# Pairwise bilinear products: one VectorE multiply over two PSUM banks, third product two halves later

## The chip, the cores and the metric

The kernel runs on one core of a Trainium2 chip. The metric is the time of one execution in microseconds on the device; lower is better. TensorE (PE in the profile) does the matrix products and writes PSUM, ScalarE (ACT) and VectorE (DVE) read and write PSUM and SBUF, GpSimd (POOL) works in SBUF, and the DMA moves data between HBM and SBUF. DMAs are issued from the queues of SyncE (SP), ScalarE and GpSimd.

## The reference

There are 1024 rows with 32 fields of 128 numbers each. For each of the 496 pairs of fields i < j there is a 128 x 128 matrix; field i is multiplied by it, and the result is multiplied element by element with field j. Everything is float32.

```python
# r_inputs: (1024, 32, 128), L0_rec_W: (496, 128, 128)
_pairs = list(itertools.combinations(range(32), 2))
v_i = inputs[:, I_IDX, :]
v_j = inputs[:, J_IDX, :]
transformed = jnp.einsum('bpd,ped->bpe', v_i, W)
return transformed * v_j
```

## The kernel before

**Tiles.** Each field is held transposed, 128 partitions (d) by 1024 columns (the rows of the batch). A pair q has one 128 x 128 weight and an output of 128 x 1024. It is worked in two halves of 512 columns; u = 2q + h numbers the halves. One half's product fills one PSUM bank (128 x 512 float32), and there are eight banks: `ppool` holds eight tiles of one bank each.

**Order of pairs.** Pairs run row by row from i = 30 down to i = 0, and in a row over j = i+1 to 31, so the first rows are short and the last is 31 pairs long.

**Three products.** The first 15 pairs (`nq0`) use one float32 matmul per half (line 209). All others use three quicker fp32r products. A weight w is split into a high part `wh`, a rest `wl` and a difference `wd`, and a field into `xh`, `xl` and `xd`. Half u goes through these steps:

1. `first(u)`: two matmuls on TensorE into its bank, `wh` by `xh` and `wl` by `xl` (line 212); then ScalarE scales the bank in place by 1 + 2^-12 (line 213).
2. `second(u)`, which runs LAG = 3 halves later in the order: the third matmul, `wd` by `xd`, adds to the bank (line 221); then VectorE multiplies the bank with field j and writes the output tile (line 227).

**The loop.** The order of all instructions is written out by hand (`manual_schedule`). For each u the loop calls `first(u)`, loads that fall due, `second(u - LAG)`, stores that fall due, and, at odd u, at most one split; the `xd` subtractions put down in `later` come last. Each engine works its instructions in this order; a wait holds up everything behind it on that engine.

**Splits.** `split_w` takes two pairs' weights at a time (128 x 256): ScalarE makes `wh` (line 127), GpSimd makes `wl` and `wd` (lines 128 to 130), in four buffers per kind. `split_x` takes half a field: ScalarE `xh` (line 142), GpSimd `xl` (lines 143 and 144), and `xd` either on GpSimd (line 148) or, for 16 fields, on VectorE through `later` (line 265), due at `min(u + XDLAG, 2*first_q[f] + LAG - 1)`.

**Output.** Four pairs share an output tile (2 MB, `out_tile`). There are seven slots for such tiles at first: three of their own (`s0` to `s2`) and four that will later hold groups of fields (`g0` to `g3`). These four are given up one after the other, ahead of the group loads at pairs 52, 141, 219 and 313 (20 pairs earlier each); from then on three are left. VectorE can't write a tile before the store that last used its slot has landed. A full tile is stored by one DMA from ScalarE's queue (line 258), SLAG = 2 halves after `second` of its last half in the order; the first four pairs and the last four are stored pair by pair, and the last two pairs in halves.

**Loads.** Weights come eight pairs at a time (512 KB, line 118) into three buffers, fields singly (512 KB, line 90) or in groups of four (2 MB, line 108), nearly all from SyncE's queue. Seven of the later weight loads go out in two parts, 112 partitions from GpSimd's queue and 16 from SyncE's (lines 102 and 103), with small DMAs (`mark`, line 99) around them.

Of the kernel before, what the change touches and what calls it, by code (L numbers as in the profile page):

```python
# [7 lines left out]
F32 = mybir.dt.float32  # L8
F32R = mybir.dt.float32r
ALU = mybir.AluOpType  # L10

P = 128
NF = 32
NQ = NF * (NF - 1) // 2
BT = 1024
HB = 512
WC = 2
WL = 8
OG = 4
EPS = 2.0**-12  # L20
NATIVE = 5
SHARED = 16
XDLAG = 10
LAG = 3
WB = 3
WLEAD = 12
XAFTER = 54
# [7 lines left out]
XAT = (313, 219, 141, 52)  # L35
OWAIT = 20
SLAG = 2


def _pairs():  # L40
# [5 lines left out]
def kernel(  # L46
# [22 lines left out]
    nc = tc.nc  # L69
# [5 lines left out]
    rpool = ctx.enter_context(tc.tile_pool(name="wr", bufs=WB))  # L75
    wpool = ctx.enter_context(tc.tile_pool(name="ws", bufs=4))
    opool = ctx.enter_context(tc.tile_pool(name="o", bufs=1))
    ppool = ctx.enter_context(tc.tile_pool(name="ps", bufs=8, space=bass.MemoryType.PSUM))

    x_sb = {}  # L80

    def load_x(f, pieces=1, eng=None):
        if f == 0:

            t = rpool.tile([P, WL, P], F32, tag="w", name="x_0").rearrange("p q e -> p (q e)")
        else:
            t = xpool.tile([P, BT], F32, tag=f"x{f}", name=f"x_{f}")
        s = BT // pieces
        for k in range(pieces):
            (eng or nc.sync).dma_start(out=t[:, k * s : (k + 1) * s], in_=xt[f, :, k * s : (k + 1) * s])  # L90
        x_sb[f] = t

    w_raw = {}
# [18 lines left out]
    def load_w(c, splits=(0, WL), eng=nc.sync):  # L112
# [4 lines left out]
        for a, b in zip(splits, splits[1:]):  # L117
            eng.dma_start(out=w_raw[c][:, a:b, :], in_=wt[c, :, a:b, :])

    w_s = {}  # L120

    def split_w(c, u):

        k = c * WC % WL
        raw = w_raw[c * WC // WL][:, k : k + WC, :].rearrange("p q e -> p (q e)")
        h, l, d = [wpool.tile([P, WC * P], F32R, tag=t, name=f"{t}_{c}") for t in ("wh", "wl", "wd")]
        nc.scalar.mul(h, raw, 1.0 - 2.0**-13)  # L127
        nc.gpsimd.tensor_tensor(l, raw, h.bitcast(F32), ALU.subtract)  # L128
        nc.gpsimd.tensor_scalar(d, h.bitcast(F32), EPS, 1.0, ALU.mult, ALU.mult)  # L129
        nc.gpsimd.tensor_tensor(d, l.bitcast(F32), d.bitcast(F32), ALU.subtract)  # L130
        w_s[c] = (h, l, d)

    x_s = {}
    later = []

    def split_x(f, a, u):
# [8 lines left out]
        if f > NF - 2 - NATIVE - SHARED:  # L145
            later.append((min(u + XDLAG, 2 * first_q[f] + LAG - 1), d, h.bitcast(F32), l.bitcast(F32)))
        else:
# [9 lines left out]
    for c in range(c0, nchunk):  # L157
        todo.append(((c - 3) * WC + 1, max(c * WC, nq0), lambda u, c=c: split_w(c, u)))
# [33 lines left out]
    def out_tile(g):  # L192
        t = min((t for t in used if (g + 1) * OG <= until.get(t, NQ + OG)), key=used.get)
        used[t] = g
        pool = xpool if t in until else opool
        return pool.tile([P, OG, BT], F32, tag=t, name=f"ot_{g}")

    ctx.enter_context(tc.manual_schedule())
    po, ots, stores = {}, {}, []


    def first(u):
        q, h = divmod(u, 2)
        i, c = pairs[q][0], q // WC
        r = slice(q % WC * P, (q % WC + 1) * P)
        s = slice(h * HB, (h + 1) * HB)
        po[u] = ppool.tile([P, HB], F32, tag="po", name=f"po_{u}")
        if q < nq0:
            nc.tensor.matmul(po[u], w_raw[q // WL][:, q % WL, :], x_sb[i][:, s], start=True, stop=True)  # L209
        else:  # L210
            for t in (0, 1):
                nc.tensor.matmul(po[u], w_s[c][t][:, r], x_s[i][t][:, s], start=t == 0, stop=t == 1)  # L212
            nc.scalar.mul(po[u], po[u], 1.0 + EPS)  # L213

    def second(u):
        q, h = divmod(u, 2)
        i, j = pairs[q]
        r = slice(q % WC * P, (q % WC + 1) * P)
        s = slice(h * HB, (h + 1) * HB)
        if q >= nq0:  # L220
            nc.tensor.matmul(  # L221
                po[u], w_s[q // WC][2][:, r], x_s[i][2][:, s], start=False, stop=True, skip_group_check=True
            )
        g, k = divmod(q, OG)
        if k == 0 and h == 0:
            ots[g] = out_tile(g)
        nc.vector.tensor_tensor(ots[g][:, k, s], po.pop(u), x_sb[j][:, s], ALU.mult)  # L227
        if q >= NQ - 2:
            stores.append((u + SLAG, out[g, :, k, s], ots[g][:, k, s]))
        elif g == 0 or q >= NQ - OG:  # L230
            if h == 1:
                stores.append((u + SLAG, out[g, :, k], ots[g][:, k]))
        elif k == OG - 1 and h == 1:
            stores.append((u + SLAG, out[g], ots[g]))

    for u in range(2 * NQ + LAG + SLAG):
        q = u // 2
        if u < 2 * NQ:
            i, j = pairs[q]
            if u % 2 == 0 and j == i + 1 and XG * ngroup < i - 2 - XLEAD:  # L240
                load_x(i - 2 - XLEAD)
            first(u)
            if u == 2 * nq0:
                move_on(5)
            if u % 2 == 0 and q in group_at:
                load_group(group_at[q])
            if u % 2 == 1 and q in w_at:
                load_w(w_at[q])
                if w_at[q] in WAPART:
                    back.append(q + BACK)  # L250
            if u % 2 == 0 and q in back:
                move_on(16 - NE if q < w_q[WAPART[-1]] else 13)
            if u == 2 * x_at + 1:
                load_x(0)
        if LAG <= u < 2 * NQ + LAG:
            second(u - LAG)
        while stores and stores[0][0] <= u - LAG:
            nc.scalar.dma_start(*stores.pop(0)[1:])
        if u % 2 == 1:
            ready = [t for t in todo if t[0] <= q]  # L260
            if ready:
                ready[0][2](u)
                todo.remove(ready[0])
        while later and later[0][0] <= u:
            nc.vector.tensor_tensor(*later.pop(0)[1:], ALU.subtract)  # L265
# [33 lines left out]
```

## Time and profile before

| | |
|---|---|
| runs | 754.4, 752.0, 750.39, 753.91 us; median 752.95 |
| profiled execution | 754.4 us in all, span 752.6 us |
| mean granted TensorE clock | 0.984 of full speed |
| DMA | 310.05 MB, mean 412 GB/s; HBM written 260.05 MB, read 49.29 MB |
| stores | 122 of 2048 KB, 13.4 us from issue to landing in the median |
| weight loads from SyncE | 54 of 512 KB, 10.8 us |
| field group loads | 4 of 2048 KB, 18.7 us |
| ScalarE xh (line 142) | 52 operations, 32.6 us |
| GpSimd wl, wd (lines 128 to 130) | 3 x 241 operations, 758, 416 and 740 ns |
| longest waits | wl on wh 78.1 us (78 times); scaling on products 54.0 (44); multiply on stores 45.7 (33) |

The span is the time from the first to the last instruction of the profiled execution; the other runs have only a total. A group's row gives how often it ran, its busy time, the mean duration of one, the idle time of the engine just ahead of it and what ended most of that idle time. Matmuls overlap: one lasts 0.39 us in the records, while they start 0.23 us apart. So TensorE's busy share is not its distance from a limit. Idle time of an engine that something else holds up costs nothing by itself.

### The profile page before, as it was taken

The numbers are of one execution on the slowest core, as the hardware profiler recorded it, in microseconds if no ns is written. First come the engines' busy times: TensorE is split into PE (matmuls) and PEld (weight loads), VectorE is DVE, ScalarE is ACT, GpSimd is POOL, SyncE is SP. The second block draws the span as 40 slices with busy tenths as digits, with TensorE's granted clock in tenths as the row PEclk, the third lists the DMA queues.
The fourth block names the chain that finished last, engine by engine and source line by source line (L and its number), as shares of the span: only waits on it lengthen the run. The fifth ranks groups of instructions, "written<-read, shape, count | busy, mean of one in ns | idle before, by whom it ended". The sixth has DMA issues, their size and how long they took to land.

```text
span 752.6 us, 10976 instructions
## 1 busy us (share of the span) xinstructions
PE 703.5 (93%) x2946; PEld 554.9 (74%) x2946; DVE 655.4 (87%) x1024; ACT 625.5 (83%) x1256; POOL 591.5 (79%) x866
## 2 busy tenths in 40 slices
PE   7998999999999997998999979989999999998994
PEld 3576777778888776776787758768777787777883
DVE  3999999999998995977889859879898989887995
ACT  1298989999999987787898868889998898887993
POOL 1789999999988788486988866878888979796761
PEclk9999999999999999899999998999999999999998
DMA  9999999999999999999999997999999999999998
GB/s 345 425 425 429 412 428 426 428 423 426 426 416 428 426 429 427 398 419 422 412 429 404 417 391 299 391 432 426 420 418 428 403 427 402 427 426 395 392 430 353
DMA packets 31789, 310.05 MB, mean 412 GB/s; under 512 B 3952, under 2 KB 4080, under 8 KB 15600
## 3 DMA queue, kind: packets, MB, share of 16 engines
q10 hardware_dynamic: 19584, 261.10, 82.5%
q1 hardware_dynamic: 10880, 45.03, 15.2%
q0 software_dynamic: 1264, 3.22, 1.3%
q8 instruction: 24, 0.39, 0.2%
q14 instruction: 37, 0.30, 0.1%
HBM read 49.29 MB, written 260.05 MB: 411 GB/s over the span
## 4 chain that ended last, share of the span: by engine, by line
PE 55%; DMA 22%; POOL 11%; DVE 8%; issue 2%; ACT 1%; DVEq 0%; ACTq 0%; POOLq 0%
PE po L212 35%; DMA out_dram<-ot 22%; PE po L221 17%; DVE ot L227 7%; PE po L209 4%; POOL xl L143 2%; POOL wl L128 2%; POOL xd L148 2%; POOL wd L130 2%; POOL xl L144 1%; POOL wd L129 1%; DVE xd L265 1%; DMA x<-in_xt_dram 1%; ACT po L213 0%; ACT wh L127 0%
## 5 line engine op out<-in xcount | busy, mean ns | idle before, releaser
L213 ACT ACTIVATE po<-po 128x512 f32<-128x512 f32 x962 | 545.2, 583 | 94.9 <-PE po L212 54.0
L227 DVE TENSOR_TENSOR ot<-po,x 128x512 f32<-128x512 f32 x720 | 459.4, 683 | 69.9 <-DMA out_dram<-ot 39.4
L212 PE MATMUL po<-xh,wh 128*128 128x512 f32 x962 | 380.4, 395 | 22.0 <-DVE ot L227 21.9
L212 PE MATMUL po<-xl,wl 128*128 128x512 f32 x962 | 378.9, 394 | 11.0 <-POOL wl L128 9.7
L221 PE MATMUL po<-xd,wd 128*128 128x512 f32 x962 | 376.9, 392 | 1.8 <-DVE xd L265 0.9
L128 POOL TENSOR_TENSOR wl<-w,wh 128x256 fp32r<-128x256 f32 x241 | 182.6, 758 | 81.4 <-ACT wh L127 78.1
L212 PEld LDWEIGHTS po<-xh,wh 128*128 128x128 f32 x962 | 182.0, 189 | 70.7 <-DVE ot L227 32.2
L212 PEld LDWEIGHTS po<-xl,wl 128*128 128x128 f32 x962 | 182.1, 189 | 54.1 <-POOL wl L128 15.5
L221 PEld LDWEIGHTS po<-xd,wd 128*128 128x128 f32 x962 | 182.0, 189 | 41.0 <-ACT po L213 2.4
L130 POOL TENSOR_TENSOR wd<-wl,wd 128x256 fp32r<-128x256 f32 x241 | 178.3, 740 | 20.1
L227 DVE TENSOR_TENSOR ot<-po,x_g 128x512 f32<-128x512 f32 x272 | 172.1, 684 | 18.5 <-PE po L212 7.5
L129 POOL TENSOR_SCALAR wd<-wh 128x256 fp32r<-128x256 f32 x241 | 100.2, 416 | 20.4
L127 ACT ACTIVATE wh<-w 128x256 fp32r<-128x256 f32 x241 | 99.3, 413 | 7.2 <-DVE ot L227 5.4
L143 POOL TENSOR_TENSOR xl<-x_g,xh 128x512 fp32r<-128x512 f32 x32 | 41.4, 1295 | 0.0
L143 POOL TENSOR_TENSOR xl<-x,xh 128x512 fp32r<-128x512 f32 x20 | 26.3, 1314 | 16.2 <-ACT xh L142 16.0
L144 POOL TENSOR_SCALAR xl<-xl 128x512 fp32r<-128x512 f32 x52 | 34.9, 671 | 4.6
L209 PE MATMUL po<-x,w 128*128 128x512 f32 x60 | 30.4, 669 | 4.0 <-DMA x<-in_xt_dram 4.0
L265 DVE TENSOR_TENSOR xd<-xh,xl 128x512 fp32r<-128x512 f32 x32 | 30.2, 944 | 0.0
L209 PEld LDWEIGHTS po<-x,w 128*128 128x128 f32 x60 | 12.4, 212 | 21.3 <-issue 14.0
L148 POOL TENSOR_TENSOR xd<-xh,xl 128x512 fp32r<-128x512 f32 x20 | 25.9, 1293 | 1.7
L142 ACT ACTIVATE xh<-x 128x512 fp32r<-128x512 f32 x20 | 12.4, 628 | 11.5 <-DMA x<-in_xt_dram 11.4
L142 ACT ACTIVATE xh<-x_g 128x512 fp32r<-128x512 f32 x32 | 20.2, 630 | 0.0
(7 smaller groups left out, 11.2 us busy)
## 6 DMA issues: line engine op xcount, KB each, us to landing
out_dram<-ot ACTq DMA_DIRECT2D x122, 2048.0 KB, 13.4
w<-in_wt_dram SPq DMA_DIRECT2D x54, 512.0 KB, 10.8
x_g<-in_xt_dram SPq DMA_DIRECT2D x4, 2048.0 KB, 18.7
x<-in_xt_dram SPq DMA_DIRECT2D x14, 512.0 KB, 9.5
w<-in_wt_dram POOLq DMA_DIRECT2D x7, 448.0 KB, 11.8
out_dram<-ot ACTq DMA_DIRECT2D x6, 512.0 KB, 8.1
x<-in_xt_dram ACTq DMA_DIRECT2D x4, 256.0 KB, 5.8
out_dram<-ot ACTq DMA_DIRECT2D x4, 256.0 KB, 6.1
```

What stands on the lines that cost most here:

```text
L127: nc.scalar.mul(h, raw, 1.0 - 2.0**-13)
L128: nc.gpsimd.tensor_tensor(l, raw, h.bitcast(F32), ALU.subtract)
L129: nc.gpsimd.tensor_scalar(d, h.bitcast(F32), EPS, 1.0, ALU.mult, ALU.mult)
L130: nc.gpsimd.tensor_tensor(d, l.bitcast(F32), d.bitcast(F32), ALU.subtract)
L143: nc.gpsimd.tensor_tensor(l, x_sb[f][:, s], h.bitcast(F32), ALU.subtract)
L144: nc.gpsimd.tensor_scalar(l, l.bitcast(F32), 1.0 / EPS, 1.0, ALU.mult, ALU.mult)
L148: nc.gpsimd.tensor_tensor(d, h.bitcast(F32), l.bitcast(F32), ALU.subtract)
L209: nc.tensor.matmul(po[u], w_raw[q // WL][:, q % WL, :], x_sb[i][:, s], start=True, stop=True)
L212: nc.tensor.matmul(po[u], w_s[c][t][:, r], x_s[i][t][:, s], start=t == 0, stop=t == 1)
L213: nc.scalar.mul(po[u], po[u], 1.0 + EPS)
L221: nc.tensor.matmul(po[u], w_s[q // WC][2][:, r], x_s[i][2][:, s], start=False, stop=True, skip_group_check=True)
L227: nc.vector.tensor_tensor(ots[g][:, k, s], po.pop(u), x_sb[j][:, s], ALU.mult)
```

## The change

PSUM tiles become pairs: `ppool` holds PB = 4 tiles of 128 x 1024 float32, two banks each, taken at the pair's first half. The matmuls and the scaling still work on one half, in its bank. VectorE no longer multiplies each half; at the pair's second half it multiplies all 1024 columns in one instruction. The last two pairs keep one multiply per half. LAG goes from 3 to 2, so the third product and all that hangs on LAG in the loop (the multiply, the due times of stores and of `xd` subtractions) come one half earlier in the order.

Because a tile now has two banks, waits between instructions on different halves of one tile are declared needless (`declare_no_dep`, through the helper `apart`): the second half's products against the scaling of the first half, and the third product of a half against the scaling of the other half. Two more are declared: the scaling against the multiply that freed its tile (the products ahead of it have waited for that), and `wh` against the `wh` four splits before it (one engine writes both).

```diff
-LAG = 3
+LAG = 2
+PB = 4
...
-    ppool = ctx.enter_context(tc.tile_pool(name="ps", bufs=8, space=bass.MemoryType.PSUM))
+    ppool = ctx.enter_context(tc.tile_pool(name="ps", bufs=PB, space=bass.MemoryType.PSUM))
...
+    scaled, taken, halved = {}, {}, {}
+
+    def apart(inst, other, reason="the halves of a pair lie in two banks"):
+
+        if other is not None:
+            tc.declare_no_dep(inst.ins, other.ins, reason=reason)
...
-        nc.scalar.mul(h, raw, 1.0 - 2.0**-13)
+        halved[c] = nc.scalar.mul(h, raw, 1.0 - 2.0**-13)
+        apart(halved[c], halved.get(c - 4), "one engine writes both, in order")
...
-        po[u] = ppool.tile([P, HB], F32, tag="po", name=f"po_{u}")
+        if h == 0:
+            po[q] = ppool.tile([P, BT], F32, tag="po", name=f"po_{q}")
         if q < nq0:
-            nc.tensor.matmul(po[u], w_raw[q // WL][:, q % WL, :], x_sb[i][:, s], start=True, stop=True)
+            nc.tensor.matmul(po[q][:, s], w_raw[q // WL][:, q % WL, :], x_sb[i][:, s], start=True, stop=True)
         else:
             for t in (0, 1):
-                nc.tensor.matmul(po[u], w_s[c][t][:, r], x_s[i][t][:, s], start=t == 0, stop=t == 1)
-            nc.scalar.mul(po[u], po[u], 1.0 + EPS)
+                m = nc.tensor.matmul(po[q][:, s], w_s[c][t][:, r], x_s[i][t][:, s], start=t == 0, stop=t == 1)
+                apart(m, scaled.get(u - 1) if h else None)
+            scaled[u] = nc.scalar.mul(po[q][:, s], po[q][:, s], 1.0 + EPS)
+            apart(scaled[u], taken.get(q - PB), "TensorE's products, which this waits for, have waited for it")
...
-            nc.tensor.matmul(
-                po[u], w_s[q // WC][2][:, r], x_s[i][2][:, s], start=False, stop=True, skip_group_check=True
+            m = nc.tensor.matmul(
+                po[q][:, s], w_s[q // WC][2][:, r], x_s[i][2][:, s], start=False, stop=True, skip_group_check=True
             )
+            apart(m, scaled[u ^ 1])
...
-        nc.vector.tensor_tensor(ots[g][:, k, s], po.pop(u), x_sb[j][:, s], ALU.mult)
+        if q >= NQ - 2:
+            nc.vector.tensor_tensor(ots[g][:, k, s], po[q][:, s], x_sb[j][:, s], ALU.mult)
+        elif h == 1:
+            taken[q] = nc.vector.tensor_tensor(ots[g][:, k, :], po.pop(q), x_sb[j], ALU.mult)
```

More of the change, by code (lines that the diff above doesn't have):

```diff
@@ L37 @@
 SLAG = 2
+PB = 4
 def _pairs():
```

## The prediction, made before the changed kernel ran

> **What bounds the kernel now.** I read the page first (busy time, slices, chain), then the groups by line, the waits, and last the stretches around the places where the DMA falls off.
>
> ```profile
> span 752.6 us, 10976 instructions
> ...
> PE 703.5 (93%) x2946; PEld 554.9 (74%) x2946; DVE 655.4 (87%) x1024; ACT 625.5 (83%) x1256; POOL 591.5 (79%) x866
> ...
> DMA  9999999999999999999999997999999999999998
> GB/s 345 425 425 429 412 428 426 428 423 426 426 416 428 426 429 427 398 419 422 412 429 404 417 391 299 391 432 426 420 418 428 403 427 402 427 426 395 392 430 353
> ...
> PE 55%; DMA 22%; POOL 11%; DVE 8%; issue 2%; ACT 1%; DVEq 0%; ACTq 0%; POOLq 0%
> ```
>
> All engines are near full, but only one resource is full in 38 of 40 slices: the DMA, at some 425 GB/s. 310.05 MB at 428 GB/s (the slices that run undisturbed) are 724 us. A group of four pairs writes 2.10 MB and needs 0.26 MB of weights: 2.36/0.428 = 5.51 us. In the timeline at 165 us TensorE's first products of successive halves start at 165.52, 166.20 and 166.88, so a half takes 0.68 us and a group 5.44. TensorE is thus 0.07 us per group faster than the DMA, and its 55% of the chain are mostly stretches in which both are full.
>
> ```profile
> L213 ACT ACTIVATE po<-po 128x512 f32<-128x512 f32 x962 | 545.2, 583 | 94.9 <-PE po L212 54.0
> L227 DVE TENSOR_TENSOR ot<-po,x 128x512 f32<-128x512 f32 x720 | 459.4, 683 | 69.9 <-DMA out_dram<-ot 39.4
> L221 PE MATMUL po<-xd,wd 128*128 128x512 f32 x962 | 376.9, 392 | 1.8 <-DVE xd L265 0.9
> L127 ACT ACTIVATE wh<-w 128x256 fp32r<-128x256 f32 x241 | 99.3, 413 | 7.2 <-DVE ot L227 5.4
> L265 DVE TENSOR_TENSOR xd<-xh,xl 128x512 fp32r<-128x512 f32 x32 | 30.2, 944 | 0.0
> ...
> DVE ot L227 <- DMA out_dram<-ot: 45.7, 33, 7.1
> PEld po L212 <- DVE ot L227: 32.2, 27, 5.8
> PE po L212 <- DVE ot L227: 21.9, 16, 5.4
> ```
>
> VectorE needs 2 x 0.683 = 1.37 us per pair where TensorE needs 1.36: once late, it never catches up. But what makes it late is, above all, an output tile whose store hasn't landed (45.7 us), and TensorE's waits on VectorE follow from that.
>
> ```profile
> 448.00:450.00 2.00, 0.04 (x1) 0.04 (x1) 0.78 (x2) 0.00 (x0) 0.00 (x0) 0.82 1.02 438
> 450.00:452.00 2.00, 2.00 (x5) 1.61 (x6) 2.00 (x4) 0.58 (x1) 0.00 (x0) 0.50 0.29 123
> 452.00:454.00 2.00, 2.00 (x7) 1.51 (x6) 1.59 (x3) 0.80 (x2) 0.00 (x0) 0.50 0.14 57
> 454.00:456.00 2.00, 2.00 (x6) 1.61 (x5) 1.20 (x2) 1.26 (x3) 0.00 (x0) 0.50 0.06 25
> ...
> 688.00:690.00 2.00, 0.37 (x2) 0.00 (x0) 0.33 (x1) 0.99 (x3) 1.24 (x3) 1.00 1.04 446
> 690.00:692.00 2.00, 1.59 (x6) 1.31 (x7) 2.00 (x4) 0.61 (x2) 1.11 (x2) 0.91 1.02 434
> 692.00:694.00 2.00, 2.00 (x6) 1.52 (x6) 2.00 (x5) 1.14 (x2) 0.00 (x0) 0.50 0.98 418
> 694.00:696.00 2.00, 2.00 (x8) 1.61 (x7) 1.46 (x3) 1.37 (x3) 0.49 (x1) 0.74 0.58 246
> ```
>
> After the bounds (start to end, us) these columns are length, then PE, PEld, DVE, ACT, POOL busy, the granted clock, the DMA's share and GB/s. Here the DMA runs dry. VectorE waits 7.10 us for a store until 449.22, TensorE stands still from 444.8 to 449.96, comes back at half clock until 456, and until then nothing new is stored. A smaller case follows a stop of 2.04 us at 688.
>
> **The change, part by part.**
>
> *One multiply per pair (494 of 496 pairs).* No row has a VectorE operation 1024 wide. The bounds: at most two narrow ones, 2 x 0.683 = 1.37 us; at least what ScalarE's two widths suggest (256 wide 413 ns, 512 wide 583, hence 243 fixed), 1.37 - 0.24 = 1.12. I take the middle, 1.24: 0.13 x 494 = 62 us less VectorE work (0 to 120). [...] Worth on the path: the chain gives line 227 7%, 53 us, so 53 x 0.13/1.37 = 5.0 us if nothing else bound there. The cover is the DMA, full in those slices; a faster VectorE only comes earlier to a tile that is still being stored. I take 0, and -5.0 as the end.
>
> *PSUM held in pairs.* From the third product of half u to the first of u+8 there are 13 matmuls before and after, 13 x 0.227 = 2.95 us. Minus the matmul (0.39) and the multiply, the spare is 1.88 us before and 2.95 - 0.39 - 1.24 = 1.32 after. And when TensorE does stand, it is released 0.56 us later. The waits count 27 stops (weight loads; the matmuls' 16 are among the same stops): 27 x 0.56 = 15 us of TensorE if uncovered. Against this, three whole pairs instead of five halves are ready when VectorE is released, and it works them off at 1.24 per pair: the group is done after about 4 x 1.24 = 5.0 us instead of 8 x 0.68 = 5.4. So output after a stop comes 0.4 us earlier, though TensorE resumes later. Net for the DMA: -0.4 us at each place where it is dry, two such places in the stretches above: -0.8. Between stops TensorE's lateness is covered by the queue of stores.
>
> *Third product two halves later.* ScalarE's scaling must end before the third product: 10 matmuls lie between before, 7 after. 10 x 0.227 - 0.39 - 0.58 = 1.30 us spare, then 0.62. Taken over the whole timeline the spare is 1.26 in the median, under 1.0 for 114 of 962 halves and under 0.68 for 12. Those come where a weight split (413 ns) or x split (630 ns) goes between scalings. TensorE would stop there by 0.1 to 0.3 us, 114 x 0.15 = 17 us at most, 12 x 0.3 = 4 at least. Spread over 120 groups that is 0.03 to 0.14 us each, beside 0.07 of TensorE's margin and its 35 us of standing: covered, apart from the end. I take +0.5 (0 to +5).
>
> *Stores.* Their issue stands on ScalarE's queue behind the scaling of half u+4 instead of u+5 and waits for the multiply. From the third product to that scaling's end are 5 x 0.227 + 0.39 + 0.58 = 2.1 us; the multiply ends after 0.39 + 0.683 before, after 0.39 + 1.24 now: spare 1.0, then 0.5. If VectorE is later (an xd of 0.94 ahead of it, 32 times), the scalings behind the issue are late, and then TensorE's third product: 32 x 0.44 = 14 us at most, all before 306 us where the DMA is full; 0. The xd's due time moves one half earlier with the same cover. Otherwise the store leaves 0.68 - 0.56 = 0.1 us earlier: -0.1 at the end, where the last two pairs stay in halves.
>
> *Waits declared needless.* ScalarE's 600 wait instructions on line 213 take 17 ns each while the scaling ahead still runs; fewer of them saves 0. The others only keep the two banks of a pair apart, as separate tiles did: 0.
>
> **Sum.** 0 - 0.8 + 0.5 - 0.1 = -0.4 against the span of 752.6. That execution took 754.4 in all; the median of the runs is 752.95. With a lean toward the bounds that are gains: I take -1 on the median, 752.
>
> [...] The half clock from 691.6 to 695.0 came after a stop of 2.04 us. [...]
>
> **Rivals.**
> Faster: the quicker group after a stop ends the dry spells. For it: the DMA's shares 0.75, 0.95, 0.96 and 0.96 of its slices (18.8 us) against 1.01 leave (0.26 + 0.06 + 0.05 + 0.05) x 18.8 = 7.9 us. Against it: 3 of 4 pairs of that group wait for TensorE at half clock, which the change doesn't touch. All of it: 752.95 - 7.9 = 745.
>
> [...]
>
> Not what it says: if the halves still wait for each other, the first products of a pair's second half wait for the first half's scaling, some 0.39 + 0.58 - 0.23 = 0.7 us per pair, 481 x 0.7 = 340 us: 1090. The declarations name exactly these pairs.
>
> **Numbers.** No change 0.44, faster rival 0.28, slower rival 0.26, not what it says 0.02. About 0.5% (3.8 us) is what a measurement of this kernel can tell from no change. The first case by itself spans 748 to 757 and gives 0.38 within, 0.03 on each side; the faster rival, 743 to 750, gives 0.27 faster and 0.01 within; the slower, 756 to 765, 0.25 slower and 0.01 within. Together faster 0.30, same 0.40, slower 0.30. The range takes in most of both rivals: 743 to 761.
>
> **What would show it.** Line 227's wide rows near 1240 ns and VectorE's busy time near 593 us; its waits on stores well above 45.7 us (the saved time turns up there); DMA still 9 in nearly every slice. Third products that wait on ScalarE: up from 3.3 us to between 4 and 17. Right if the dry spell after the last change of tiles is there again, 0.4 us shorter. Wrong if the number of half-clock stretches before the end is not three, or if slices show the DMA idle while TensorE waits for ScalarE.

## The result and the profile after

The changed kernel takes 750.26 us in the median of 43 runs (749.38 to 754.32), the kernel before 753.37 in 64 runs beside them (749.8 to 755.83). The ratio is 0.9974, 95% interval 0.9966 to 0.9983: 2 us less, as the means have it (752.75 and 750.82 us; the medians lie 3.1 apart), and inside the 0.5% that the prediction called no change. The single executions of each kernel scatter by more than that: of the kernel before, 18 of 64 took less than 751 us and 42 more than 752.5, of the changed kernel 28 of 43 less than 751 and 5 more than 752.5. The profiled execution of the changed kernel (750.29 us) has a span of 748.5 us, 4.1 less than that of before (754.4 us).

First the page of the changed kernel (span, busy time, the DMA's slices, the chain by engine):

```profile
span 748.5 us, 10410 instructions
...
PE 711.1 (95%) x2946; PEld 545.4 (73%) x2946; DVE 619.6 (83%) x530; ACT 637.2 (85%) x1256; POOL 594.1 (79%) x866
...
DMA  9999999999999999999999998999999999999998
GB/s 340 432 419 433 405 430 426 428 427 412 425 398 433 427 428 425 428 427 423 428 418 405 427 407 318 384 427 426 418 401 426 418 425 405 414 434 423 426 428 346
...
PE 71%; DMA 11%; POOL 9%; DVE 3%; issue 2%; ACT 2%; ACTq 0%; POOLq 0%; DVEq 0%
```

The DMA is full as before, still with one dip (318 GB/s, slice 25). VectorE works 36 us less, but TensorE's and ScalarE's busy time went up, by 8 and 12 us. The chain has moved from the DMA (22% to 11%) to TensorE (55% to 71%).

The groups and the waits that answer to those shown of before (lines 223, 225, 234 and 244 are the former 212, 213, 221 and 227):

```profile
L225 ACT ACTIVATE po<-po 128x512 f32<-128x512 f32 x962 | 555.5, 584 | 65.1 <-PE po L223 52.1
L244 DVE TENSOR_TENSOR ot<-po,x 128x1024 f32<-128x1024 f32 x358 | 431.8, 1221 | 88.6 <-DMA out_dram<-ot 26.7
...
DVE ot L244 <- PE po L234: 37.1, 109, 1.1
DVE ot L244 <- DMA out_dram<-ot: 35.7, 26, 5.5
PEld po L234 <- ACT po L225: 17.1, 48, 1.6
PEld po L223 <- DVE ot L244: 15.8, 11, 4.4
...
PE po L223 <- DVE ot L244: 11.2, 9, 4.0
...
PE po L234 <- ACT po L225: 3.2, 6, 0.8
```

The lines of before that these are read against, as far as the prediction doesn't show them:

```profile
DVE ot L227 <- PE po L221: 16.8, 20, 1.8
...
PEld po L221 <- ACT po L213: 2.4, 3, 1.3
...
PE po L221 <- ACT po L213: 0.9, 1, 0.9
```

A wide multiply takes 1.22 us. VectorE waits less for stores than before (35.7 us against 45.7) and more for third products (37.1 against 16.8). TensorE waits for ScalarE, weight loads and matmuls together, 20.3 us instead of 3.3. Last the stretches around the one long dry spell, with the columns as before:

```profile
452.00:454.00 2.00, 2.00 (x6) 1.54 (x5) 0.85 (x2) 1.13 (x3) 0.00 (x0) 0.50 0.08 33
454.00:456.00 2.00, 2.00 (x10) 1.66 (x9) 1.68 (x2) 1.70 (x5) 1.40 (x3) 1.00 0.94 393
```

The spell is there again, but it ends two microseconds sooner: the DMA is back at 393 GB/s from 454 to 456, where before it moved 25.

### The profile page after: what moved, and what is told of

The parts are those of the page before. It is cut to its first block, busy times and chain, and to the rows that moved or that the text cites. A ratio compares the mean times of both kernels' runs of the same rounds, so it can differ in the third digit from the quotient of the medians.

```text
span 748.5 us, 10410 instructions
## 1 busy us (share of the span) xinstructions
PE 711.1 (95%) x2946; PEld 545.4 (73%) x2946; DVE 619.6 (83%) x530; ACT 637.2 (85%) x1256; POOL 594.1 (79%) x866
## 4 chain that ended last, share of the span: by engine, by line
PE 71%; DMA 11%; POOL 9%; DVE 3%; issue 2%; ACT 2%; ACTq 0%; POOLq 0%; DVEq 0%
PE po L223 44%; PE po L234 23%; DMA out_dram<-ot 11%; PE po L220 4%; DVE ot L244 2%; POOL wd L140 2%; POOL wl L138 2%; POOL xl L153 2%; POOL xd L158 1%; ACT po L225 1%; POOL wd L139 1%; POOL xl L154 1%; DMA x<-in_xt_dram 1%; DVE xd L282 1%; DVE ot L242 0%
## 5 line engine op out<-in xcount | busy, mean ns | idle before, releaser
L225 ACT ACTIVATE po<-po 128x512 f32<-128x512 f32 x962 | 555.5, 584 | 65.1 <-PE po L223 52.1
L244 DVE TENSOR_TENSOR ot<-po,x 128x1024 f32<-128x1024 f32 x358 | 431.8, 1221 | 88.6 <-DMA out_dram<-ot 26.7
L234 PE MATMUL po<-xd,wd 128*128 128x512 f32 x962 | 385.1, 400 | 7.6 <-ACT po L225 3.2
L138 POOL TENSOR_TENSOR wl<-w,wh 128x256 fp32r<-128x256 f32 x241 | 179.7, 746 | 74.0 <-ACT wh L136 70.9
L140 POOL TENSOR_TENSOR wd<-wl,wd 128x256 fp32r<-128x256 f32 x241 | 182.3, 757 | 20.1
L244 DVE TENSOR_TENSOR ot<-po,x_g 128x1024 f32<-128x1024 f32 x136 | 163.9, 1222 | 31.2 <-PE po L234 10.9
L139 POOL TENSOR_SCALAR wd<-wh 128x256 fp32r<-128x256 f32 x241 | 103.8, 431 | 20.4
L153 POOL TENSOR_TENSOR xl<-x,xh 128x512 fp32r<-128x512 f32 x20 | 25.8, 1290 | 16.6 <-ACT xh L152 16.3
L154 POOL TENSOR_SCALAR xl<-xl 128x512 fp32r<-128x512 f32 x52 | 32.8, 631 | 4.5
L282 DVE TENSOR_TENSOR xd<-xh,xl 128x512 fp32r<-128x512 f32 x32 | 26.4, 826 | 0.0
```

Source lines behind the costliest of these rows:

```text
L153: nc.gpsimd.tensor_tensor(l, x_sb[f][:, s], h.bitcast(F32), ALU.subtract)
L154: nc.gpsimd.tensor_scalar(l, l.bitcast(F32), 1.0 / EPS, 1.0, ALU.mult, ALU.mult)
L225: scaled[u] = nc.scalar.mul(po[q][:, s], po[q][:, s], 1.0 + EPS)
L234: m = nc.tensor.matmul(po[q][:, s], w_s[q // WC][2][:, r], x_s[i][2][:, s], start=False, stop=True, skip_group_check=True)
L244: taken[q] = nc.vector.tensor_tensor(ots[g][:, k, :], po.pop(q), x_sb[j], ALU.mult)
```

## The experiments

Each run was timed beside runs of the kernel before on the same chip.

**1. LAG = 2 alone.** On the kernel before:

```diff
-LAG = 3
+LAG = 2
```

> The kernel before with LAG = 2 alone: eight tiles of one bank, one multiply per half. Theory 'dry spells' (the DMA sets the time; the wide multiply lets VectorE work off what has piled up behind a store, so less of the DMA is unused): the gain needs the wide multiply, so 752.5 to 754, ratio 0.999 to 1.001. Rival 'earlier' (the third product one half earlier brings all results and stores forward): the whole gain is here, 750 to 751, ratio 0.997.

751.94 us, ratio 0.9991 (0.9976 to 1.0007). That is the side of "dry spells", but the interval overlaps the changed kernel's (0.9966 to 0.9983), so this run doesn't exclude that LAG alone gives a part of the gain. Of use is a wait: TensorE waits for ScalarE 17.0 us here, with no pair tiles. So it is LAG = 2 that takes ScalarE's spare time.

**2. Pair tiles with narrow multiplies.** The changed kernel, with

```diff
-        if q >= NQ - 2:
-            nc.vector.tensor_tensor(ots[g][:, k, s], po[q][:, s], x_sb[j][:, s], ALU.mult)
-        elif h == 1:
-            taken[q] = nc.vector.tensor_tensor(ots[g][:, k, :], po.pop(q), x_sb[j], ALU.mult)
+        taken[u] = nc.vector.tensor_tensor(ots[g][:, k, s], po[q][:, s], x_sb[j][:, s], ALU.mult)
```

and the third product declared apart from the other half's multiply (the declaration on the scaling goes by halves too).

> The changed kernel with one multiply per half again, on its pair tiles and at LAG = 2. Dry spells: no gain, 753 to 755, ratio 1.000 to 1.002, VectorE busy near 655 us again. Earlier: 750 to 751, ratio 0.997. A second thing is seen here: in the changed kernel the scaling of a pair's second half waits for the scaling of the first (back to back they start 0.62 us apart, 0.56 and less before); it is here too, so if it costs anything, this is slower than LAG = 2 alone by that, up to 2 us.

752.83 us, ratio 1.0005 (0.9987 to 1.0022). Without the wide multiply the pair tiles give nothing. ScalarE's busy time is 637.6 us, as in the changed kernel; with LAG = 2 on one-bank tiles it is 627.0. The extra 10 us are a wait that the pair tiles bring: the scaling of the second half waits for the scaling of the first, on the same engine. In ScalarE's timeline two scalings back to back took, for example, this before and after the change (start, length, what):

```profile
656.91 1.07 ACT L213 ACTIVATE po<-po 128x512 f32<-128x512 f32 x2
```

```profile
655.25 1.21 ACT L225 ACTIVATE po<-po 128x512 f32<-128x512 f32 x2
```

Over the whole trace, 675 scalings directly follow another one. Before the change 8 of them start 0.60 to 0.64 us after it, in the changed kernel 286, here 288.

**3. The wide multiply with LAG = 3.** The changed kernel, with `LAG = 3`.

> The changed kernel with LAG = 3: ScalarE has 0.68 us more spare time before the third product, PSUM has 0.68 us less (2.27 - 0.39 - 1.22 = 0.66 us). Dry spells: the wide multiply is there, so most of the gain is: 750 to 752, ratio 0.997 to 0.999; TensorE's waits on ScalarE fall from 20 us to under 5, those on VectorE rise from 27 us to 35 and more. Earlier: no gain, 753, ratio 1.000.

752.4 us, ratio 1.0004 (0.9987 to 1.0021). A miss for "dry spells" as I had it: the wide multiply is there and the gain is not. TensorE's waits moved as expected (on ScalarE 4.4 us, on VectorE 52.0, 57.6 with the last pairs). So the wide multiply doesn't give the 2 us by itself, and LAG = 2 with pair tiles (experiment 2) doesn't either.

**4. Splits between a pair's scalings.** The changed kernel, with

```diff
-        if u % 2 == 1:
+        if u % 2 == 0:
             ready = [t for t in todo if t[0] <= q]
```

and the second scaling declared apart from the first where a split stands between them.

> The changed kernel with the weight and field splits at the first half of a pair, so that ScalarE has another operation between a pair's two scalings in 286 of 481 pairs, and the wait of the second scaling for the first costs nothing there. Dry spells: that wait costs TensorE but not the DMA, so 749.5 to 751, ratio 0.997 as the changed kernel, with TensorE's waits on ScalarE below 20 us. Rival 'ScalarE is on the path now': the 20 us of those waits are partly on the path, and it gains 2 us or more, 748 and below, ratio 0.994.

749.26 us, ratio 0.9951 (0.9931 to 0.9971). This is the lowest time of the kernels that store the whole output, and falls between the two expectations. TensorE's waits on ScalarE are 11.9 us, and ScalarE's busy time is back at 627.0 us, as without pair tiles.

**5 and 6. Half of the stores.** In both kernels each store of a group and of a pair writes 512 of the 1024 columns:

```diff
-            stores.append((u + SLAG, out[g], ots[g]))
+            stores.append((u + SLAG, out[g, :, :, :HB], ots[g][:, :, :HB]))
```

> The kernel before, but every store of a pair writes only 512 of its 1024 columns; the rest of the output is left out (the last two pairs are stored whole). The output's 260 MB become 131. If the DMA sets the time, it falls to what VectorE and TensorE need: VectorE 992 x 0.672 + 30 = 697 us plus the first 9 us and some waits, 710 to 722, ratio 0.945 to 0.96. If TensorE, ScalarE or VectorE set it, it stays at 745 and above, ratio over 0.99. VectorE's waits on stores go to nearly 0.

> The changed kernel with the same cut (512 of 1024 columns stored per pair). With the DMA out of the way the change is worth what its engines need: VectorE 494 x 1.22 + 26 = 630 us no longer binds; TensorE and ScalarE do, 962 halves of 0.69 to 0.70 after the first 33 us and 5 at the end, 702 to 712, so 5 to 15 us less than the kernel before with the cut. If the saved VectorE time were on no path even so, both are within 3 us of each other.

The kernel before falls to 719.82 us, ratio 0.9566 (0.9535 to 0.9598), as expected of a kernel that the DMA bounds. The changed kernel falls only to 737.06 us, 0.9797 (0.977 to 0.9824). My estimate for it was at least 25 us too low, and on the wrong side: with the DMA out of the way (250 GB/s over the span in the first, 245 in the second) the change costs 17 us, far more than the four runs of each scatter (718.85 to 721.05 and 736.67 to 738.11). Two of the longest waits of this run:

```profile
DVE ot L244 <- PE po L234: 59.8, 198, 1.1
...
PEld po L234 <- ACT po L225: 19.8, 51, 2.0
```

VectorE waits for third products and third products wait for ScalarE, 25.1 us with the matmuls' own 5.3. In the run of before with the same stores these are 16.6 and 3.3 us. So the faster multiply sits behind third products that wait for scalings. These waits don't add up to the 17 us, though: TensorE's waits on GpSimd's `wl` go the other way (35.5 us before, 15.1 after), and how much of the 17 us ScalarE causes isn't shown.

**7. The place of the splits alone.** The kernel before, with `u % 2 == 0`.

> The kernel before with nothing changed but the place of the splits (at the first half of a pair instead of the second). If that place is what helps by itself, 751 and below, ratio 0.997 to 0.998. If it helps only by covering the wait between a pair's scalings, which the kernel before doesn't have, 752.5 to 753.5, ratio 0.999 to 1.001.

751.66 us, ratio 0.9996 (0.9976 to 1.0016): by itself the place does nothing that can be told.

**8. LAG = 2 and that place, without pairs.** The kernel before, with both edits.

> The kernel before with LAG = 2 and the splits at the first half of a pair: one-bank tiles, narrow multiplies. Against the changed kernel with the same split place (749.26 us, 0.9951) it lacks only the wide multiply. Dry spells with the wide multiply needed: 751.5 to 753, ratio 0.998 to 1.000. Rival 'the wide multiply is worth nothing, LAG and the place of the splits do it': 749 to 750, ratio 0.995 to 0.996.

749.67 us, ratio 0.9959 (0.9943 to 0.9976). The rival was right: at this place of the splits, one-bank tiles and narrow multiplies reach the same as experiment 4.

**9 and 10. Where the store stands.** The kernel before with `SLAG = 1`, and the changed kernel with `SLAG = 3`: each gets the other's place of the store on ScalarE's queue.

> The kernel before with SLAG = 1: a group's store stands behind the scaling of half u+4 on ScalarE's queue, where LAG = 2 puts it too, and nothing else moves. Theory 'store behind the scalings' (after a wait the next store can't leave until TensorE, at half clock, has made the products that the scaling ahead of it needs, and the DMA is dry so long): half the gain or more, 751 to 752.5, ratio 0.997 to 0.999, and from the freed tile to the next store at about 449 us some 6 us instead of 7.2. Rival 'the third product's place': no gain, 753 to 754, ratio 1.000.

> The changed kernel with SLAG = 3: the store stands behind the scaling of half u+5 again, as in the kernel before. Store behind the scalings: the gain shrinks to half or less, 751.5 to 753, ratio 0.998 to 1.000, and from a group's first multiply to its store it is 5.6 us in the median instead of 5.4. Rival 'a store that waits for VectorE holds up ScalarE, and that costs': it gets better, 749 to 750, ratio 0.995 to 0.996.

The changed kernel with the store later loses its gain: 752.58 us, 0.9997 (0.9979 to 1.0014). The kernel before with the store earlier is at 752.59 us, 0.9994 (0.9978 to 1.001): no gain that can be told. Yet in one profile of each the dry spell changed as expected (with the store earlier it is 5.4 us from the freed tile to the store, at 449.0 and 454.4 us). ScalarE's timeline shows how the first store after the spell leaves. In the profiles before the change, after it, and after it with the store later (start, length, what, idle time ahead of it):

```profile
456.31 0.58 ACT L213 ACTIVATE po<-po 128x512 f32<-128x512 f32 x1 [0.35 <-PE po L212]
456.37 0.34 ACTq L258 DMA_DIRECT2D out_dram<-ot  x1
```

```profile
453.45 0.58 ACT L225 ACTIVATE po<-po 128x512 f32<-128x512 f32 x1 [0.76 <-PE po L223]
453.48 0.34 ACTq L275 DMA_DIRECT2D out_dram<-ot  x1
```

```profile
454.36 0.58 ACT L225 ACTIVATE po<-po 128x512 f32<-128x512 f32 x1 [0.76 <-PE po L223]
...
455.38 0.58 ACT L225 ACTIVATE po<-po 128x512 f32<-128x512 f32 x1
455.45 0.34 ACTq L275 DMA_DIRECT2D out_dram<-ot  x1
```

In the first two the store is issued right behind a scaling that had waited for products made at half clock, in the third behind the scaling after such a one and a `wh`. VectorE's first multiply into the freed tile starts at 449.2, 448.1 and 447.9 us, so from there to the store it is 7.2, 5.4 and 7.5 us. The multiplies of the group had ended at 454.9, 452.7 and 453.4: the store then stood 1.5, 0.8 and 2.0 us behind scalings that had nothing to do with it.

**11 and 12. Both kernels once more.**

> The kernel before once more, for a second profile: if the half-clock stretches and the dry spells belong to the kernel and not to one execution, there are three again, near 299, 449 and 690 us, two of them 6.8 us long, and some 8 us of the DMA are unused between 440 and 480 us.

> The changed kernel once more, for a second profile: if they belong to the kernel, two half-clock stretches of 3.4 us near 341 and 450 us, none near 299 and 690, and some 6.5 us of the DMA unused between 440 and 480 us.

753.5 and 749.97 us. Half-clock stretches: before again two of 6.8 us, at 300 and 447 us, where three were expected; after again one of 6.8 at 340 and one of 3.4 at 449 us. So those near 299 (before only), 340 (after only) and 449 us came again. They aren't bound to the pair tiles or to LAG, however: the changed kernel with the store later has one of 6.8 us at 301 us and none near 340, the kernel before with the earlier store has ones of 3.4 us at 303 and 341. The one at 691 us, which the prediction counted on, didn't come again. From the first multiply into the freed tile to the store these second profiles show (VectorE and ScalarE's queue, before again, then after again):

```profile
449.08 4.41 DVE L227 TENSOR_TENSOR ot<-po,x 128x512 f32<-128x512 f32 x7 [7.10 <-DMA out_dram<-ot]
455.29 0.34 ACTq L258 DMA_DIRECT2D out_dram<-ot  x1
```

```profile
447.22 3.49 DVE L244 TENSOR_TENSOR ot<-po,x 128x1024 f32<-128x1024 f32 x3 [3.95 <-DMA out_dram<-ot]
453.00 0.34 ACTq L275 DMA_DIRECT2D out_dram<-ot  x1
```

That is 6.2 and 5.8 us: the store leaves 0.4 us sooner, where the first profiles have 1.8.

The stretch from 440 to 480 us, in six profiles, one fence each: before, before again, after, after again, before with the store earlier, after with the store later. The last column is GB/s.

```profile
440.00:480.00 40.00, 33.66 (x135) 26.92 (x134) 29.89 (x46) 28.90 (x59) 26.39 (x39) 0.91 0.85 341
```

```profile
440.00:480.00 40.00, 33.66 (x139) 27.08 (x138) 30.84 (x47) 29.66 (x60) 27.28 (x41) 0.91 0.86 346
```

```profile
440.00:480.00 40.00, 35.33 (x145) 27.70 (x144) 29.05 (x24) 31.53 (x63) 28.53 (x43) 0.96 0.91 355
```

```profile
440.00:480.00 40.00, 36.90 (x152) 28.97 (x151) 30.57 (x26) 32.85 (x66) 29.96 (x45) 0.96 0.94 370
```

```profile
440.00:480.00 40.00, 34.89 (x146) 28.11 (x145) 31.99 (x49) 31.08 (x63) 28.65 (x43) 0.96 0.91 368
```

```profile
440.00:480.00 40.00, 34.43 (x137) 26.87 (x136) 27.30 (x24) 29.70 (x59) 26.79 (x40) 0.91 0.84 338
```

Against 428 GB/s, (428 - x)/428 x 40 us of the DMA go unused here: 8.1 and 7.7 us before, 6.8 and 5.4 after, a difference of 1.8 us in the mean (1.3 in the first profiles, 2.3 in the second). That is the size of the gain (0.0026 x 753.4 = 2.0). In the 440 us ahead of it all four profiles of the two kernels have 418 or 419 GB/s, and from 480 to 720 us 416 and 421 before, 420 and 419 after. With the place of the store swapped it is 5.6 us for the kernel before and 8.4 for the changed one. The other kernels agree in part: with the store behind half u+4, LAG = 2 alone 5.9, narrow pairs 7.3, experiments 4 and 8 7.2 each; behind u+5, the wide multiply at LAG = 3 7.9, but the splits alone 6.7.

Another reading of these numbers stands beside the store's place. Both profiles of the kernel before are of executions above 752.5 us (754.4 and 753.5), both of the changed kernel of executions below 751 (750.29 and 749.97). Leaving out experiments 4 and 8, the five profiles with 7.3 us and more unused are of executions of 752.6 us and more, the five with 6.8 us and less of executions of 751.4 us and less. The unused time thus goes with the time of the single execution at least as well as with the kernel or with the place of its store. No profile is of an execution of the kernel before below 751 us, so these can't be told apart.

## Why the prediction came out as it did

The forecast, 752 us and no change within 0.5%, holds. Its frame was right, most of its terms were not. That most errors of its terms don't show in the time is the cover of the full DMA, which it had put first; that the lean toward a gain came out is luck, since the terms it rested on didn't hold. By a sign that it named itself, a number of half-clock stretches other than three, it was wrong.

- **The DMA bounds the kernel**: shown by experiments 5 and 6. The time that VectorE saved was worth next to nothing under the full DMA (experiment 3: ratio 1.0004).
- **The wide multiply, 1.24 us**: it takes 1.22. But the 62 us of saved work were 36. I multiplied 494 pairs by twice the mean of 683 ns, while back to back those narrow operations overlap (459.4 us busy for 720 of them, 638 ns each).
- **"VectorE's waits on stores well above 45.7 us"**: wrong, 35.7 and in the second profile 28.6. The saved time turned up as waits for third products, 37.1 us instead of 16.8, so ScalarE and TensorE became the later ones.
- **PSUM held in pairs, TensorE released later**: the 15 us of added stops didn't come. TensorE waited less for VectorE, 27.0 us against 54.1 as weight loads and matmuls together. That goes with LAG and not with the tiles: 25.2 us with LAG = 2 alone, 52.0 with the wide multiply at LAG = 3.
- **Third product two halves later**: TensorE's waits on ScalarE are 20.3 us, above the 4 to 17 I gave, and while the DMA is full next to nothing of it shows in the time. The cost without that cover is 17 us by experiments 5 and 6, for the whole change; they don't tell LAG from the new wait.
- **"The others only keep the two banks of a pair apart, as separate tiles did: 0"**: this step failed. The pair tile brings a wait that separate tiles didn't have, between the two scalings on ScalarE itself, and none of the declarations names it. In the rows shown it makes two scalings in a row 1.21 us long instead of 1.07, and it adds some 10 us to ScalarE's busy time.
- **Stores, -0.1, and dry spells, -0.8**: the sizes were off, and which mechanism gives the 2 us is open. I took the quicker multiply for the cause and reckoned the store's place at full clock, where a half is 0.68 us. After the long stop a half takes 1.28 us, and in the changed kernel the store waits for one half fewer. With a shorter stop (4.0 and 2.4 us against 5.2 and 5.2) and a half-clock stretch of 3.4 instead of 6.8 us the store there leaves 1.8 us sooner in the first profiles, but only 0.4 in the second. The second place, at 690 us, was there in one profile only.
- **Rivals**: the faster one put all dry spells at 7.9 us; a gain of a quarter of that was measured, and it isn't shown to come from them. No run shows the 3 to 12 us that the slower one (756 to 765 us), and with it the upper end of the range, puts on the 752.95 us of before: no execution of the changed kernel took more than 754.32 us, and its profile has two half-clock stretches before the end instead of three (the second profiles of both kernels have two each). The shorter spare time in PSUM (1.32 us against 1.88, as the prediction reckons it) cost nothing that shows, since TensorE waited less for VectorE.

Shown: the DMA bound; that the changed kernel is the slower one without it; that pair tiles make the second scaling wait for the first; that the gain goes when the store goes back to its former place (0.9997, though the interval touches the changed kernel's). Not shown: where the 2 us come from. The place of the store is a candidate, but the kernel before keeps no gain with the earlier store, though the dry spell in its profile is some 2 us shorter; one of its other slices is lower (392 GB/s in the fifth, against 412 and 427 before), and its profile has a half-clock stretch at 57 us that neither kernel has. And every comparison of dry spells is of one or two executions, while the executions of one kernel scatter by more than 2 us. Why LAG = 2 and the other place of the splits give 0.995 to 0.996 together and nothing that can be told alone is open as well: the two profiles lie at 7.2 us of unused DMA at the dry spell, no better than the changed kernel's, and have no one place where the rest is won.

## What to carry to other kernels

Before making an engine faster, cut the traffic of the resource that is full and time both versions: here the version with the faster multiply was 17 us behind once the DMA no longer hid it. When work gets merged into bigger tiles, look for the waits that the merge adds between an engine's own instructions, and not only for those between engines. A store on a compute engine's queue leaves only behind the work ahead of it there (here 0.8 to 2.0 us after its data were ready, at the dry spell); look at that place, and time it, before speeding up what makes the data. And when a gain is smaller than the scatter of single executions, profile several of each kernel before explaining it by one profile of each. For this kernel the version to keep is that of experiment 4 or 8 (749.3 and 749.7 us), though neither is told apart from the other, and both intervals overlap the changed kernel's.

## What the runs showed of the hardware

TensorE's granted clock fell to 0.50 of full speed after some of its stops, and their length alone doesn't tell which. Stops of 2.04 us (before, at 688 us) and 2.42 us (after again, at 446 us) were followed by 3.4 us at half clock, and stops of 2.49 (before, at 338 us) and 2.13 us (after, at 491 us) were not. Ahead of the last 15 us the stretches in these four profiles were 3.4 or 6.8 us long: 6.8 after stops of 5.2 and 5.4 us (before), 3.4 after 3.0 and 4.0 us (after), but 6.8 after one of 3.1 us (after again). With half of the stores, where TensorE never stopped for as long as 1.8 us after the first 35 us, no stretch at half clock stands in either profile before the last 6 us (mean granted clock 0.997 before, 0.998 after).
